# Two queues and some row operations rearranged in a graph-attention and top-p diffusion kernel

## The chip, the cores and the metric

The kernel runs on one core of a Trainium2 chip. A core has a matrix engine (PE, with its weight loads shown apart as PEld), a vector engine (DVE), an activation engine (ACT), a general-purpose engine (POOL, also called GpSimd) and SP, which here only issues transfers. Each engine takes its instructions from its own queue in order, and a wait of one instruction holds what stands behind it. The metric is device time in microseconds (us) of one execution; the median of several runs is compared.

## The reference

There are N = 4096 nodes with 256 features and a dense 0/1 matrix `adj`. Layer 0 is a graph attention layer of four heads; layer 1 is a diffusion with two operators, a fixed graph walk R and an attention that keeps the largest probabilities of each row until they sum to 0.9. Both are applied to the normalised input and added to it:

```python
R = S + jnp.eye(N)
R = R / R.sum(-1, keepdims=True)
Z = jnp.zeros_like(X); Xf = X; Xa = X
for n in range(2):
    A = _top_p_attention(Xa, W1, W2, W3)
    Xf = R @ Xf
    Xa = A @ Xa
    Z = Z + Xf @ U1[n].T + Xa @ U2[n].T
h = X + Z
...
return (h - mu) / jnp.sqrt(var + LN_EPS) * ln_g + ln_b

# around it
h = jnp.maximum(_layernorm(x), 0.0)
x = x + _L0_gnn_ref(h, adj, W, a, gamma, beta)
h = jnp.maximum(_layernorm(x), 0.0)
x = x + _L1_gnn_ref(h, adj, W1, W2, W3, U1, U2, ln_g, ln_b)
```

The final result is the layer-0 output x (called x1 in the kernel) plus the normalised h times `ln_g` plus `ln_b`.

## The kernel before

The nodes form NB = 32 row blocks of 128. The program's order is written out by hand: in each `manual_schedule` every engine's instructions stand in the order of the source, so what precedes what on a queue can be read off the code.

**Layer 0** (to about 780 us) makes the projections of all blocks and then 16 passes, one for each group of G0 = 8 blocks and each head. After the last head of a group comes `closing` (L495): statistics, then `close(i)` once per block, then `relu`, one piece at a time between the pair products of later passes (and, for the last group, between the first products of hop 1). `close` normalises the attention output into a tile `ob`, adds it to the block of `X` on DVE (L512) and stores `X` to `x1_d` from POOL's queue (L513). `ob` shares two buffers with `hb` of the prologue. POOL also adds `beta_r` to each block once (L627).

**Hop 1 and hop 2** are the products R @ Xf with the graph matrix, 128 products each (four passes of 32). `order[n]` names the n-th. For each one the kernel needs a row block, split into a high and a low part by ACT and DVE (`split`, L467 and L468, five buffers `hl`), and the matching edges (`edge`, L482, 512 KB from `adj_d`, issued by SP, five buffers). `graph_products` (L646) then issues eight matmuls of 512 columns. In hop 1 the rows are in `X`; in hop 2 `source` (L454) loads them from `xf_d`, 128 KB each, from POOL's queue (L461), into three buffers `x1` and two `xa`. `hops` (L687) lays this out: at its n-th turn it calls `source(n + 2)`, `edge(n)`, `split`, `own` and the products n - 5. `begin` does the first five of hop 2 while step 1's last block is still attended.

Hop n+1 is interleaved with two generators: `fills` makes the projections of step n (`projections`, L777), the first three blocks' exponentials (L947) and their probes (L954, then `first_step`, L968, some 20 one-column operations on POOL ending in `c3`, L997 or L1000), and `picks` does these blocks' searches on DVE (L1009, L1033 to L1052).

In the second step `projections` also calls `carried` for every block (L791): four matmuls (L797) make the products of the states with both U2 matrices; ACT copies the first half to a tile `part` (L799) and stores it in `v_d` from its own queue (L800), and DVE copies the second half into `X` (L801). `z_d` holds what step 1 left of Z plus X (stored by `finish`, L1311).

**Each step's loop** attends the blocks in turn. For block b, `chosen_kept(b)` (L1408) issues, engine by engine, the search for the threshold (DVE), `polished(b - 3)` (L1332, L1333 on POOL, store by SP), the third probe of b + 1 (L1015 on DVE, which needs `c3`), `finish(b - 2)` and `finish_scale(b - 2)` (L1313 and the statistics on DVE, L1320 to L1324 on POOL), `first_step(b + 2)`, `gathered(b - 1)` (three row operations on POOL, L1150 to L1152), `masked(b)` (L1058 on DVE), and `normal(b - 2)` on ACT. Then `began` loads a swapped copy of the queries by SP, `loads(b)` (L1109) loads xf, v, z and x1 of the block by SP, and `attend` (L1154) issues PE's work: the logits of block b + 3 (L763), 32 transposes (L1124, copied by ACT in L1126), 32 accumulations (L1132), and the product with U1 (L1142). The last three blocks have no logits to make. In step 1 the same loop runs with fewer row operations: `gathered`, `polished` and `normal` act in step 2 alone.

Of the kernel before, what the change touches and what calls it, by code (L numbers as in the profile page):

```python
# [11 lines left out]
F32 = mybir.dt.float32  # L12
# [10 lines left out]
ALU = mybir.AluOpType  # L23
# [3 lines left out]
P = 128  # L27
# [13 lines left out]
G0 = 8  # L41
# [15 lines left out]
def gat_then_top_p_diffusion(  # L57
# [18 lines left out]
    nc = tc.nc  # L76
    N, D = x.shape
    HD = a.shape[0] // 2
    H = D // HD
    DA = w2_t.shape[0]  # L80
    NB = N // P
    KC = D // P
# [32 lines left out]
    z_d = dram.tile([NB, P, D], F32, name="z_d")  # L115
    v_d = dram.tile([NB, P, D], F32, name="v_d")
# [45 lines left out]
    with tc.tile_pool(name="l0", bufs=1) as l0, tc.tile_pool(name="l0s", bufs=2) as l0s, tc.tile_pool(name="l0o", bufs=1) as l0o:  # L162
# [26 lines left out]
        with tc.manual_schedule(engines=every | {ET.SP}):  # L189
# [5 lines left out]
                nc.sync.dma_start(X[:, ts(g, 4), :], x[ts(g, 4 * P), :].rearrange("(b p) d -> p b d", p=P))  # L195

            nc.sync.dma_start(X[:, 0, :], x[:P, :])
            spots = l0.tile([P, KC, 2, H], F32, name="spots")
            nc.vector.memset(spots, 0.0)
            twice = l0.tile([2, 2, HD], F32, name="twice")  # L200
            nc.scalar.dma_start(twice, bass.AP(tensor=a.tensor, offset=a.offset, ap=[[HD, 2], [0, 2], [1, HD]]))
            nc.sync.dma_start(wx[:, :, :D], w.rearrange("(k p) d -> p k d", p=P))
            nc.sync.dma_start(X[:, 1:4, :], x[P:4 * P, :].rearrange("(b p) d -> p b d", p=P))
# [11 lines left out]
            slots = [t[:, i, :].bitcast(BF16).rearrange("p (h t w) -> p h t w", h=H, t=2) for t in slots for i in range(t.shape[1])]  # L215
            for t in slots:
                nc.gpsimd.memset(t[:, :, :, W3:], 1.0)
            roomy = l0o.tile([P, G0, D], F32, name="o").rearrange("p a b -> p (a b)")
            sr0 = l0s.tile([P, G0 * P], F32, name="sr")
            UV = 2 * H * W1  # L220
            uvs = [roomy[:, ts(i, UV)] for i in range(3)] + [l0s.tile([P, G0 * P], F32, name="sr")[:, :UV],
# [17 lines left out]
            def opened(b):  # L239
                if b < NB:  # L240
                    rs, nmr = pro.scales[b // 4] if b > 3 else pro.first
                    hb = pro.hb[b] = l0s.tile([P, D], F32, name="hb", tag="ob")
                    nc.scalar.activation(hb, X[:, b, :], AF.Relu, scale=rs[:, b % 4:b % 4 + 1], bias=nmr[:, b % 4:b % 4 + 1])

            def turned_rows(b):
# [208 lines left out]
        def source(A, n):  # L454
            if n in A.src or n >= len(order):
                return
            if A.hop == 0:
                A.src[n] = X[:, order[n][1], :]
            else:
                A.src[n] = S.rows.tile([P, D], F32, name="x1", bufs=3) if n % 5 < 3 else S.rows.tile([P, D], F32, name="xa")  # L460
                nc.gpsimd.dma_start(A.src[n], xf_d[order[n][1]])  # L461

        def split(A, n):
            while A.parted < min(n, len(order)):
# [30 lines left out]
        def closing(ig):  # L495
            o = out_rows[ig]
            mv = l0s.tile([P, G0, nc.vector.BN_AGGR_DIM], F32, name="mv8")
            scales = []

            def stats(i0):  # L500
                for i in range(i0, i0 + 2):
                    moments_of(mv[:, i, :], o[:, i, :])
                if i0 == G0 - 2:
                    scales.extend(steps(mv, G0, l0s))

            def close(i):
                b = ig * G0 + i
                xb = X[:, b, :]
                ob = l0s.tile([P, D], F32, name="ob")
                nc.scalar.activation(ob, o[:, i, :], AF.Identity, scale=scales[0][:, i:i + 1], bias=scales[1][:, i:i + 1])  # L510
                nc.vector.tensor_mul(ob, ob, gamma_r)
                nc.vector.tensor_add(xb, xb, ob)  # L512
                nc.gpsimd.dma_start(x1_d[b], xb)  # L513
                moments_of(mv[:, i, :], xb)
                if i == G0 - 1:
                    steps(mv, G0, l0s, x_rs[:, ts(ig, G0)], x_nmr[:, ts(ig, G0)])

            def relu(i0):
                for b in range(ig * G0 + i0, ig * G0 + i0 + 2):
                    nc.scalar.activation(X[:, b, :], X[:, b, :], AF.Relu, scale=x_rs[:, b:b + 1], bias=x_nmr[:, b:b + 1])  # L520
            return [lambda i=i: stats(i) for i in range(0, G0, 2)] + [lambda i=i: close(i) for i in range(G0)] \
                + [lambda i=i: relu(i) for i in range(0, G0, 2)]
# [254 lines left out]
    def projections(cur, n, G):  # L777
# [10 lines left out]
        lengths = small.tile([P, NB, 2], F32, name="lengths", bufs=1)  # L788
        u2 = S.u2.pop() if n > 0 else None

        def carried(xs, g, i):  # L791
            if n == 0:
                return
            b = 4 * g + i
            pt = ps3.tile([P, 4, P], F32, name="tp").rearrange("p a b -> p (a b)")
            for k in range(KC):
                nc.tensor.matmul(pt, xs[:, k, i, :], u2[:, k].rearrange("p n m -> p (n m)"), start=(k == 0), stop=(k == KC - 1))  # L797
            v = rows.tile([P, D], F32, name="part", bufs=3)
            nc.scalar.copy(v, pt[:, :D])  # L799
            nc.scalar.dma_start(block(v_d, b), v)  # L800
            nc.vector.tensor_copy(cur[:, b, :], pt[:, D:])  # L801

        for g in range(NB // 4):
            xs = l1e.tile([P, 3, 4, P], F32, name="xs", tag="e1")
# [301 lines left out]
    def block(t, b):  # L1106
        return t[ds(b, 1)].rearrange("o p d -> (o p) d")

    def loads(r):  # L1109
        r.xf, r.part = rows.tile([P, KC, P], F32, name="xf"), rows.tile([P, D], F32, name="part", bufs=3)  # L1110
        nc.sync.dma_start(r.xf, xft_d[r.n][ds(r.b, 1)].rearrange("o p s i -> (o p) s i"))
        if r.n > 0:
            r.v = rows.tile([P, D], F32, name="xa")
            nc.sync.dma_start(r.v, block(v_d, r.b))
            nc.sync.dma_start(r.part, block(z_d, r.b))
            r.x1 = rows.tile([P, D], F32, name="x1", bufs=3)
            nc.sync.dma_start(r.x1, block(x1_d, r.b))
        r.acc = ps1.tile([P, 2, D], F32, name="acc")
        r.far = r.acc[:, 1, :]
# [27 lines left out]

    def gathered(r):
        if r.n + 1 == STEPS:
            nc.gpsimd.tensor_tensor(r.part, r.part, r.v, ALU.add)  # L1150
            nc.gpsimd.tensor_tensor(r.x1, r.x1, ln_b_r, ALU.add)
            nc.gpsimd.tensor_tensor(r.part, r.part, r.xf.rearrange("p k i -> p (k i)"), ALU.add)  # L1152

    def attend(r, cur, ahead, between={}, eT=()):  # L1154
# [175 lines left out]
    def polished(r):  # L1330
        if r.n + 1 == STEPS:
            nc.gpsimd.tensor_tensor(r.part, r.part, ln_g_r, ALU.mult)  # L1332
            nc.gpsimd.tensor_tensor(r.part, r.part, r.x1, ALU.add)  # L1333
            nc.sync.dma_start(block(out.rearrange("(b p) d -> b p d", p=P), r.b), r.part)
# [48 lines left out]
    for n in range(STEPS):  # L1383
        cur = X
# [3 lines left out]
        with tc.manual_schedule(engines=every):  # L1388
# [19 lines left out]
            def chosen_kept(b):  # L1408

                r = blocks[b]  # L1410
                if not hasattr(r, "kept"):
                    candidates(r, found)
                if b > 2:
                    polished(blocks.pop(b - 3))
                if b + 1 < NB and not hasattr(blocks[b + 1], "thirded"):
                    third_probe(blocks[b + 1])
                if b > 1:
                    finish(blocks[b - 2])
                    finish_scale(blocks[b - 2])
                if b + 2 < NB and not hasattr(blocks[b + 2], "stepped"):  # L1420
                    first_step(blocks[b + 2])
                if 0 < b < NB - 1:
                    gathered(blocks[b - 1])
                if not hasattr(r, "kept"):
                    masked(r)
                if 1 < b < NB - 1:
                    normal(blocks[b - 2])
# [77 lines left out]
```

## Time and profile before

| | |
|---|---|
| median of 3 runs | 2851.52 us (2849.42 to 2852.96) |
| the profiled execution | 2851.36 us, its span 2849.5 us |
| mean granted PE clock | 0.994 |
| busy: DVE, ACT, POOL, share of the span | 76%, 67%, 34% |
| transfers | 376.43 MB, mean 132 GB/s |

```profile
PE   6999999999999999999999999999899999999998
DVE  9867878878554485888888887343565999999997
ACT  8867977879533727777887773233427778887782
POOL 7311121111010321333223331111524766666664
DMA  9969596786376881000000002767891111111110
```

Each digit is the busy share, in tenths, of one of 40 equal slices of 71 us. Layer 0 fills about the first eleven, hop 1 the next four and a half, step 1's loop runs to the 25th, hop 2 takes the next five, and step 2's loop the rest. The transfers tell the stages apart: the loops move little, the hops much.

```profile
ar<-adj_d SPq DMA_DIRECT2D x212, 512.0 KB, 4.5
x<-xf_d POOLq DMA_DIRECT2D x78, 128.0 KB, 4.6
xa<-xf_d POOLq DMA_DIRECT2D x50, 128.0 KB, 4.6
v_d<-part ACTq DMA_DIRECT2D x32, 128.0 KB, 2.3
```

These are issues by line: destination and source, the queue, the count, the size of one and the median time from issue to landing in us.

### The profile page before, as it was taken

Reading aid. Unit: us, or ns where it says so; the run is one execution under the profiler, and the core shown is the slowest. Engines: PE = TensorE matmul, PEld = TensorE weight load, DVE = VectorE, ACT = ScalarE, POOL = GpSimd, SP = SyncE. Lnnn points to the kernel's source line nnn. Section 1 sums busy time; section 2 is a strip of 40 time slices with the busy share of each in tenths; the row PEclk is TensorE's granted clock in tenths of the full one; section 3 lists DMA queues with packets and bytes.
Section 4 is the critical chain, followed back from the end, with each engine's and each line's share of the span. In section 5 each row is a group of like instructions: output and inputs, shape, how many; then the busy total and the mean of one; then the engine's idle time right before and its main releaser. Section 6 shows DMA issues by size and latency. Waiting matters only on the chain. (4 is left out here: it accounts for less than half of the span.)

```text
span 2849.5 us, 51595 instructions
## 1 busy us (share of the span) xinstructions
PE 2794.6 (98%) x18791; PEld 2439.9 (86%) x18791; DVE 2174.8 (76%) x5067; ACT 1917.7 (67%) x3066; POOL 980.9 (34%) x2023
## 2 busy tenths in 40 slices
PE   6999999999999999999999999999899999999998
PEld 5899999999988888888888888667678888888887
DVE  9867878878554485888888887343565999999997
ACT  8867977879533727777887773233427778887782
POOL 7311121111010321333223331111524766666664
PEclk9999999999999999999999999999999999999999
DMA  9969596786376881000000002767891111111110
GB/s 208 261 234 203 215 239 183 226 187 237 116 259 200 261 303 48 25 23 20 20 20 24 23 19 82 240 194 256 272 341 47 31 36 37 31 31 31 36 35 26
DMA packets 161825, 376.43 MB, mean 132 GB/s; under 512 B 18198, under 2 KB 107158, under 8 KB 157462
## 3 DMA queue, kind: packets, MB, share of 16 engines
q1 hardware_dynamic: 124064, 254.33, 27.0%
q0 software_dynamic: 32256, 114.31, 15.5%
q10 hardware_dynamic: 5238, 4.35, 0.5%
q8 instruction: 153, 2.51, 0.4%
q14 instruction: 114, 0.93, 0.1%
HBM read 305.48 MB, written 113.57 MB: 147 GB/s over the span
## 5 line engine op out<-in xcount | busy, mean ns | idle before, releaser
L1132 PE MATMUL acc<-X,eT 128*128 128x256 f32 x4096 | 971.7, 382 | 3.6 <-ACT eT L1126 3.1
L1132 PEld LDWEIGHTS acc<-X,eT 128*128 128x128 f32 x4096 | 738.2, 190 | 111.4 <-ACT eT L1126 31.9
L400 PE MATMUL acc<-ut,m 128*128 128x195 bf16 (+1 forms) x8192 | 698.1, 246 | 1.2 <-DVE m L379 0.9
L400 PEld LDWEIGHTS <-m 128*128 128x128 fp8e4 x8192 | 696.8, 97 | 2.4 <-DVE m L379 1.4
L372 ACT ACTIVATE g<-sr,d_big 128x1024 uint8<-128x1024 f32 x448 | 473.1, 1135 | 10.0 <-DVE m L378 10.0
L947 ACT ACTIVATE e<-mm,nm 128x1024 f32<-128x1024 f32 x256 | 286.3, 1119 | 195.8 <-PE mm L763 195.4
L1126 ACT COPY eT<-tp 128x512 f32<-128x512 f32 x512 | 297.1, 581 | 90.2 <-PE tp L1124 89.8
L1033 DVE MAX8 cand<-big 128x8 f32<-128x228 f32 (+1 forms) x1152 | 348.3, 380 | 0.0
L646 PE MATMUL mm<-ar,hl 128*128 128x512 f32 x848 | 337.7, 409 | 9.7 <-ACT hl L467 3.9
L1015 DVE SCALAR_TENSOR_TENSOR big<-e,c 128x4096 f32<-128x4096 f32 x58 | 261.9, 4515 | 97.6 <-POOL c L1000 58.6
L646 PE MATMUL acc<-ar,hl 128*128 128x512 f32 x848 | 325.3, 394 | 0.0
L1124 PE MATMUL tp<-ident,e 128*128 128x128 f32 x2048 | 306.1, 272 | 1.9 <-DVE ns_i_u L920 1.0
L1124 PEld LDWEIGHTS tp<-ident,e 128*128 128x128 f32 x2048 | 254.8, 140 | 61.2 <-DVE ns_i_u L920 1.3
L378 DVE TENSOR_TENSOR m<-g,ax 128x512 uint32<-128x512 uint32 x256 | 188.8, 737 | 97.3 <-PE acc L400 76.8
L1058 DVE SCALAR_TENSOR_TENSOR e<-e,found 128x4096 f32<-128x4096 f32 x58 | 259.1, 4468 | 0.0
L954 ACT ACTIVATE void<-e,c 128x2048 int8<-128x2048 f32 x128 | 257.5, 2012 | 0.0
L954 ACT ACTIVATE void<-e,c1x 128x2048 int8<-128x2048 f32 x128 | 257.4, 2011 | 0.0
L646 PEld LDWEIGHTS mm<-ar,hl 128*128 128x128 f32 x848 | 160.3, 189 | 50.3 <-issue 10.9
L379 DVE TENSOR_TENSOR m<-m,ax 128x512 uint32<-128x512 uint32 x256 | 183.2, 716 | 25.7 <-PE acc L400 0.5
L763 PE MATMUL mm<-kT,qT 128*128 128x512 f32 x512 | 197.9, 467 | 2.2 <-ACT e L947 2.2
L646 PEld LDWEIGHTS acc<-ar,hl 128*128 128x128 f32 x848 | 160.0, 189 | 36.7 <-issue 4.1
L971 POOL TENSOR_TENSOR sums<-sums 128x2 f32<-128x2 f32 x64 | 12.8, 200 | 511.1 <-ACT void L954 511.1
(313 smaller groups left out, 3610.9 us busy)
## 6 DMA issues: line engine op xcount, KB each, us to landing
ar<-adj_d SPq DMA_DIRECT2D x212, 512.0 KB, 4.5
adj_d<-ax POOLq DMA_DIRECT2D x32, 2048.0 KB, 7.7
ut<-uv_d SPq DMA_DIRECT2D x60, 784.0 KB, 6.1
aru<-adj_d SPq DMA_DIRECT2D x44, 512.0 KB, 4.5
ax<-in_adj_t_dram POOLq DMA_DIRECT2D x32, 512.0 KB, 18.3
x<-xf_d POOLq DMA_DIRECT2D x78, 128.0 KB, 4.6
xf<-xft_d SPq DMA_DIRECT2D x64, 128.0 KB, 2.2
sr<-s_d SPq DMA_DIRECT2D x15, 512.0 KB, 4.8
```

The costliest lines, as they stand in the source:

```text
L372: nc.scalar.activation(g[:, c, :], shared[k].sr, AF.Relu, scale=BIG, bias=d_big[:, h, j:j + 1])
L400: nc.tensor.matmul(shared[k].acc[i][:, t, :cols], m[t][:, c, ts(i, P)], shared[k].ut[j // QUARTER][:, j % QUARTER, t, :cols], start=(j == ...
L646: nc.tensor.matmul(A.acc[c][s], A.hl[m][:, t, ts(s, P)], A.ar[m][:, ts(c, 512)], start=(j == 0 and t == 0), stop=(j == NB - 1 and t == 1))
L763: nc.tensor.matmul(pm[:, h, :], q[t], kT[:, ds(h * (N // 2) + c * 512, 512)], start=(t == 0), stop=(t == 1))
L947: nc.scalar.activation(ev[:, :, c, :], r.pm[c], AF.Exp, bias=r.nm, accum_out=r.sums[:, c // 2, c % 2:c % 2 + 1])
L954: nc.scalar.activation(void, r.e[:, ts(h, N // 2)], (AF.Relu, AF.Sign)[i], bias=r.c1, scale=-1.0, accum_out=r.sums[:, h, 2 + i:3 + i])
L1015: nc.vector.scalar_tensor_tensor(big, r.e, r.c3, r.e, ALU.is_le, ALU.mult, accum_out=r.low3)
L1033: nc.vector.max(cand[:, s, :], big[:, edges[s]:edges[s + 1]])
L1058: nc.vector.scalar_tensor_tensor(r.e, r.e, r.t, r.e, ALU.is_ge, ALU.mult, accum_out=kept)
L1124: nc.tensor.transpose(pt[:, i, :], r.e[:, ts(4 * g + i, P)], ident)
L1126: nc.scalar.copy(eT, pt)
L1132: nc.tensor.matmul(r.acc[:, 0, :], eT[:, i, :], cur[:, j, :], start=(j == 0), stop=(j == NB - 1))
```

## The change

The rows of hop 2 are loaded from SP's queue instead of POOL's. `carried` loads the block's z ahead (two blocks early, from POOL's queue) and adds it on DVE to the first half, so that `v_d` holds v + z; its store moves from ACT's queue to POOL's, and the copy of the second half from DVE to ACT. `loads` then fetches one tile less. `close` adds `ln_b_r` on POOL, into `ob`, and stores that, so `gathered` keeps one of its three operations. `ob` and `hb` get four buffers; `spots` and `twice` move into tiles that are there anyway. In `chosen_kept`, `polished(b - 3)` moves behind `finish_scale(b - 2)`.

```diff
-            spots = l0.tile([P, KC, 2, H], F32, name="spots")
+            roomy = l0o.tile([P, G0, D], F32, name="o").rearrange("p a b -> p (a b)")
+            spots = roomy[:, G0 * D - 2 * KC * H:].rearrange("p (c t h) -> p c t h", c=KC, t=2)
...
-            twice = l0.tile([2, 2, HD], F32, name="twice")
+            twice = sT[:2].rearrange("t (r d) -> t r d", r=2)
@@ opened
-                    hb = pro.hb[b] = l0s.tile([P, D], F32, name="hb", tag="ob")
+                    hb = pro.hb[b] = l0s.tile([P, D], F32, name="hb", tag="ob", bufs=4)
@@ source
-                nc.gpsimd.dma_start(A.src[n], xf_d[order[n][1]])
+                nc.sync.dma_start(A.src[n], xf_d[order[n][1]])
@@ close
-                ob = l0s.tile([P, D], F32, name="ob")
+                ob = l0s.tile([P, D], F32, name="ob", tag="ob", bufs=4)
...
-                nc.gpsimd.dma_start(x1_d[b], xb)
+                nc.gpsimd.tensor_tensor(ob, xb, ln_b_r, ALU.add)
+                nc.gpsimd.dma_start(x1_d[b], ob)
@@ projections
+        zs = {}
+
+        def fetched(b):
+            if n > 0 and b < NB:
+                zs[b] = rows.tile([P, D], F32, name="z", tag="xf")
+                nc.gpsimd.dma_start(zs[b], block(z_d, b))
+
+        for b in range(2):
+            fetched(b)
@@ carried
-            nc.scalar.copy(v, pt[:, :D])
-            nc.scalar.dma_start(block(v_d, b), v)
-            nc.vector.tensor_copy(cur[:, b, :], pt[:, D:])
+            nc.vector.tensor_tensor(v, pt[:, :D], zs.pop(b), ALU.add)
+            nc.gpsimd.dma_start(block(v_d, b), v)
+            fetched(b + 2)
+            nc.scalar.copy(cur[:, b, :], pt[:, D:])
@@ loads
-            r.v = rows.tile([P, D], F32, name="xa")
-            nc.sync.dma_start(r.v, block(v_d, r.b))
-            nc.sync.dma_start(r.part, block(z_d, r.b))
+            nc.sync.dma_start(r.part, block(v_d, r.b))
@@ gathered
-            nc.gpsimd.tensor_tensor(r.part, r.part, r.v, ALU.add)
-            nc.gpsimd.tensor_tensor(r.x1, r.x1, ln_b_r, ALU.add)
             nc.gpsimd.tensor_tensor(r.part, r.part, r.xf.rearrange("p k i -> p (k i)"), ALU.add)
@@ chosen_kept
-                if b > 2:
-                    polished(blocks.pop(b - 3))
...
                     finish(blocks[b - 2])
                     finish_scale(blocks[b - 2])
+                if b > 2:
+                    polished(blocks.pop(b - 3))
```

More of the change, by code (lines that the diff above doesn't have):

```diff
@@ L217, in gat_then_top_p_diffusion @@
                 nc.gpsimd.memset(t[:, :, :, W3:], 1.0)
-            roomy = l0o.tile([P, G0, D], F32, name="o").rearrange("p a b -> p (a b)")
             sr0 = l0s.tile([P, G0 * P], F32, name="sr")
```

## The prediction

> **What bounds the kernel now.** I read the page's busy table and its 40 slices first, then the windows of the slices where PE is not full, then the timelines of PE, ACT and POOL inside them, and last the groups by shape in the two long loops. PE carries the span: 98% busy, and nearly full in all but a few places.
>
> ```profile
> PE 2794.6 (98%) x18791; PEld 2439.9 (86%) x18791; DVE 2174.8 (76%) x5067; ACT 1917.7 (67%) x3066; POOL 980.9 (34%) x2023
> ```
>
> The largest hole lies in hop 2 (about 1778 to 2138 us). The windows view gives busy time and, in brackets, instructions started per stretch; then PEclk, DMA share and GB/s:
>
> ```profile
> 2020.00:2030.00 10.00, 10.00 (x45) 8.24 (x44) 8.22 (x25) 6.21 (x9) 8.76 (x20) 1.00 0.93 341
> 2030.00:2040.00 10.00, 5.17 (x19) 3.41 (x19) 5.09 (x22) 4.12 (x8) 3.89 (x11) 0.78 0.83 288
> 2040.00:2050.00 10.00, 6.64 (x24) 4.97 (x23) 2.73 (x15) 0.40 (x1) 6.69 (x15) 0.84 0.53 163
> 2050.00:2060.00 10.00, 9.44 (x30) 7.62 (x31) 9.35 (x17) 2.00 (x5) 2.73 (x5) 0.70 0.62 214
> 2060.00:2070.00 10.00, 10.00 (x45) 8.20 (x45) 9.50 (x27) 2.19 (x6) 3.28 (x6) 1.00 0.94 315
> ```
>
> A full stretch starts 45 matmuls; the three in the middle start 19, 24 and 30, and the granted clock falls with them. The timelines say who is late:
>
> ```profile
> 2028.02 0.63 POOL L461 DMA_DIRECT2D xa<-xf_d  x1
> 2033.59 0.40 ACT L467 CAST hl<-xa 128x256 fp32r<-128x256 f32 x1 [6.56 <-DMA xa<-xf_d]
> 2034.05 0.50 PE L646 MATMUL mm<-aru,hl 128*128 128x512 f32 x1 [1.80 <-ACT hl L467]
> ...
> 2036.91 0.20 POOL L971 TENSOR_TENSOR sums<-sums 128x2 f32<-128x2 f32 x1 [1.62 <-ACT void L954]
> 2044.66 1.72 POOL L461 DMA_DIRECT2D x<-xf_d  x3
> 2049.39 0.40 ACT L467 CAST hl<-x 128x256 fp32r<-128x256 f32 x1 [9.73 <-DMA x<-xf_d]
> 2050.56 0.77 PE L646 MATMUL mm<-ar,hl 128*128 128x512 f32 x1 [3.92 <-ACT hl L467]
> ```
>
> POOL runs the small operations of `first_step` (L971 to L997) from 2018.95 to 2027.9 and again from 2036.91 to 2044.6; the row loads L461 stand behind them in POOL's queue, ACT then waits 6.56 and 9.73 us for rows, and PE for ACT.
>
> The two loops over 32 row blocks are another matter. Their L1142, once per block, comes every 22.30 us in step 1 and every 22.26 us in step 2, although DVE has 47.2 us of waits for POOL over 25 blocks of step 1 (1.9 us each) and none in step 2. So PE sets both. In step 2 DVE only looks like the bound (the chain of waits follows it there): L1058 ends 2.96 us before PE takes its result, block after block. What fills it shows in the groups of step 1 (1150 to 1700 us), then of step 2 (2200 to 2750 us):
>
> ```profile
> L1045 DVE TENSOR_TENSOR_SCAN cum<-best,cum,zero 128x48 f32<-128x48 f32 x24 | 7.7, 321 | 0.9
> L1050 DVE CUSTOM_DVE_ANT_0 work<-drop,best 128x48 f32<-128x48 f32 x24 | 6.4, 268 | 0.8
> L1049 DVE TENSOR_SCALAR drop<-cum 128x48 f32<-128x48 f32 x24 | 4.6, 194 | 0.8
> ...
> L1050 DVE CUSTOM_DVE_ANT_0 work<-drop,best 128x48 f32<-128x48 f32 x25 | 19.2, 768 | 0.9
> L1045 DVE TENSOR_TENSOR_SCAN cum<-best,cum,zero 128x48 f32<-128x48 f32 x25 | 16.5, 659 | 0.9
> L1049 DVE TENSOR_SCALAR drop<-cum 128x48 f32<-128x48 f32 x25 | 14.2, 570 | 0.9
> ```
>
> The same three operations cost 0.78 us in step 1 and 2.00 in step 2, where POOL's five row operations (0.73 us each) run beside them.
>
> **What the Trainium skill says.** SBUF — State Buffer, "SBUF: two separate sides": VectorE and GpSimd share a port pair under an exclusive lock, and the loser blocks for the whole instruction. The trace agrees both ways: the groups above, and POOL's one-column L1320, which takes 4.36 us while L1058 (4.45 us) runs. DMA: Bandwidth & Descriptors, "Issuing engines are not separate DMA queues": moving a DMA to another issuer saves only the issuer's time, as all run on the same 16 engines. So I count nothing for bandwidth, only for the place in the queue. The same page, "Latency and other measured facts", puts the first byte of a DMA issued by SP or ACT near 0.6 us and of GpSimd's near 1 us; here SP's 128 KB loads land in 2.2 us in step 2 and POOL's in 3.4 (median, 1780 to 1925 us) to 5.2 (2000 to 2125 us), but under different load.
>
> **The change part by part.** *Row loads of hop 2 on SP.* 128 of L461 leave POOL. From 2031.5 to 2062 PE starts 73 matmuls; at its steady 0.2275 us (2062 to 2086: 105 in 24 us) these take 16.6 us, so 13.9 us were lost. On SP row n+2 stands ahead of the edges of n and behind those of n-1, which wait for product n-6. It is used at product n+2, so it has 7 products, 12.7 us at 8 x 0.2275 each, for landing, ACT (0.41) and DVE (0.42). POOL gave it some 15 us less whatever `first_step` took. I take the 13.9 us as won. The new wait ahead of an edge load is split n-3 on DVE (L468), 4.5 us earlier than the edge's own wait for product n-5; DVE's pieces there are at most 2.35 us (L1009), so it mostly hides. What is late next is the DMA: a product needs 640 KB, 360 GB/s at full rate, where 341 to 400 GB/s is what such stretches move; from 2086 to 2098, 43 matmuls took 12 us instead of 9.8, on edges. I keep that 2.2 us, and charge 1.0 for its spreading (0 to 4; if the whole stretch to 2098 ran at that 0.279 us, 178 x 0.0515 = 9.2).
>
> At the start of hop 2 the move costs. Before, POOL sent rows 5 to 7 at 1773.6 to 1776.3; now they follow edge 5 (1784.49), with the X load and row 8, before edge 6. Four issues at 0.43 put edge 6 1.7 us later, and PE uses it at about 1792, where its landing was the last wait. Charge 2.0 (0.5 to 3.5).
>
> *z joined to the states' products.* 32 copies on ACT (L799, 0.37) become 32 additions on DVE, nearest row L1313, 0.48; DVE's copy (L801, 0.43) goes to ACT. The store moves from ACT (L800, 0.34 of issue) to POOL, with 32 new z loads; the z loads of step 2 and 32 v loads vanish. PE is full from 1800 to 1925 with DVE at about 40% and ACT at 30%: nothing on the path. A new wait: the addition needs z, and behind it on DVE stand the hop's L468. z of b+2 is issued after addition b: 0.48 + 2 x 0.54 + 3.4 = 5.0 us, where two blocks of PE take 8.2 (four take 16.45) and the tightest pair 6.65. Cost 0 (0 to 3 for single late landings).
>
> *ln_b in layer 0.* 32 additions on POOL, 0.74 each (L627 is the same shape), and the store reads `ob`, of which there are now four. POOL is busy 5 to 25% there, its closings have 1.24 us of idle time per block even in the last eight (799 to 812 us), and DVE, which they can block for 0.74 us, is under 60% busy in that stretch while PE is 49.3 to 50 of 50 us busy. Cost 0 (-0.5 to +1). `spots` and `twice` only change places: 0.
>
> *Step 2's loop.* POOL loses two row operations a block (L1150, L1151: 1.46 us), and L1332 and L1333 move ahead of `first_step`, beside L1033. There DVE should not be blocked: L1040, the same operation, kept 0.31 us beside L1150. DVE gains up to 1.2 us a block, but PE paces, so 28 blocks give 0. `first_step` starts about 1 us later, with 4.3 us to spare before L1015. The out store and the next q and block loads behind it on SP come some 12 us later; q is used a block later and xf at the block's end (20 us on), so 0. At the end, where blocks 29 to 31 have no logits and PE needs 18.7 us, DVE is late today: PE waits 0.84 us for L1058, and 1.04 and 0.65 for eT where step 1 shows 0.29. With DVE ahead that is 0.84 + 0.75 + 0.36 = 1.95 us. Take 2.0 (0.8 to 2.2).
>
> **Sum.** 13.9 - 1.0 - 2.0 + 2.0 = 12.9 us off. The profiled execution took 2851.4 us (span 2849.5); the median of the runs is 2851.5, so both say **2838.5 us**. With all bounds good (13.9 + 2.2 - 0.5 + 2.2 + 0.5) it is 2833; with all bad (13.9 - 4 - 3.5 + 0.8 - 4) 2848.
>
> **Rivals.**
> *The transfers take over.* Rows and edges in one queue, at 360 GB/s wanted, run at the rate of 2086 to 2098: the 9.2 us above instead of 1.0, so 2846.7. For it: DMA share 0.93 to 1.03 from 2060 to 2120. Against: PE started 45 or 46 in most of these stretches all the same.
> *Nothing is won in hop 2*, as SP's in-order queue waits on DVE's splits and edges come late as rows did: only the tail's 2.0 less the start's 2.0, so 2851.5. Against: 4.5 us of slack.
> *Slower: the z loop.* If a z load lands in L, two blocks take 1.56 + L; from L = 6.7 it is slower than PE's 8.2, and at about 7.5 it eats all the gain. At L = 8.5 it costs 0.92 x 32 = 29 us, so 2868. For it: one row load of POOL landed in 6.6 there, and under 2000 to 2125's load up to 8.5. Against: the median of 3.4.
> *The DVE slack counts in the loop:* if PE did follow DVE in step 2, 28 x 1.2 = 34 us would go (2805). Step 1, where DVE waits and PE's period is the same, speaks against it.
>
> **How the numbers follow.** Forecast 0.76; transfers 0.10; nothing won 0.03; z loop 0.08; loop follows DVE 0.03. The range 2831 to 2847 holds most of the forecast with its bounds, and the transfers' case. A change under 0.2% (5.7 us, so from 2845.8 up) can't be told from none. Faster is 0.75 of the forecast (0.01 lies in its bad end), 0.06 of the transfers' case and the loop's 0.03: 0.84. Same: 0.01, 0.04 and 0.02 of nothing won, 0.07. Slower: the z loop and 0.01 of nothing won, 0.09.
>
> **What would show it.** Right: no ACT wait for a row over 2 us in hop 2, PEclk 1.00 in its slices, 45 matmuls per 10 us, L1142 still every 22.26 to 22.30 us, L1049 near 0.2 us, DVE waiting for L997. Wrong: PE idle for edges, L468 waiting behind a z, a loop period under 22.2.

## The result, and the profile after

| | before | after |
|---|---|---|
| median (lowest to highest) | 2851.5 us (2849.4 to 2855.6), 6 runs | 2840.0 us (2838.8 to 2842.5), 6 runs |
| ratio, 95% interval | | 0.996 (0.9947 to 0.9972) |
| span of the profiled execution | 2849.5 us | 2837.2 us |
| mean granted PE clock | 0.994 | 0.996 |

The change takes off 11.5 us, where 12.9 were forecast. To find where, I compare positions in the two traces. They are start times of single matmuls, in us from the start of the span; the last column is what the stretch since the row above gained (+) or lost (-).

| matmul | before | after | stretch |
|---|---|---|---|
| first product of layer 0 (L400) | 79.64 | 80.08 | -0.44 |
| last product of hop 1 | 1072.91 | 1075.09 | -1.74 |
| first product of hop 2 | 1778.03 | 1779.92 | +0.29 |
| last product of hop 2 | 2137.84 | 2126.89 | +12.84 |
| U1 product of block 28 in step 2's loop (the fourth last) | 2782.03 | 2770.87 | +0.21 |
| U1 product of block 31 | 2835.32 | 2822.74 | +1.42 |
| end of the span | 2849.50 | 2837.18 | -0.26 |

Hop 2 gained 12.84 us and the tail 1.42; layer 0 with hop 1 lost 1.74. The 0.44 at the very start is not from the change: the kernel with the row loads alone, whose layer 0 is that of before, has its first product at 80.12.

The busy table of the page after:

```profile
PE 2790.7 (98%) x18791; PEld 2438.5 (86%) x18791; DVE 2155.8 (76%) x5067; ACT 1915.4 (68%) x3066; POOL 915.8 (32%) x1927
```

POOL has 96 instructions fewer: 128 row loads and 64 row operations are gone, 64 z loads and v stores and 32 row operations came. PE is still the bound, and the hole in hop 2 is filled. These are the windows of after (columns as in the prediction: stretch, PE, PEld, DVE, ACT, POOL, PEclk, DMA share, GB/s):

```profile
2030.00:2040.00 10.00, 10.00 (x46) 8.21 (x45) 8.05 (x33) 3.92 (x7) 6.81 (x20) 1.00 0.95 336
2040.00:2050.00 10.00, 10.00 (x45) 8.23 (x44) 9.66 (x25) 2.44 (x6) 0.19 (x1) 1.00 1.01 375
2050.00:2060.00 10.00, 10.00 (x45) 8.23 (x44) 10.00 (x26) 2.04 (x5) 0.00 (x0) 1.00 1.02 353
```

Where before started 19, 24 and 30 matmuls, after starts 46, 45 and 45, at full clock. The waits view of ACT in after from 2000 to 2070 us (engine, line, releaser: total, times, longest):

```profile
ACT hl L467 <- DMA x<-xf_d: 13.0, 10, 2.3
...
ACT hl L467 <- DMA xa<-xf_d: 6.3, 5, 1.7
```

The longest wait for a row in this stretch is 2.3 us, where it was 9.7. ACT still waits 15 times for rows, but PE is busy all through 2020 to 2060 us, so each row arrives before PE asks for it. `first_step` still keeps POOL busy (6.8 us of 10 in 2030 to 2040), and no row load stands behind it. The transfers themselves did not get faster: the page after has a median of 5.1 us from issue to landing, where POOL's loads took 4.6.

In step 2's loop the groups of after (2200 to 2750 us; POOL's L1009 makes `c3`) show DVE's three small operations back at step 1's price, 2.00 us down to 0.80, and the third probe L1027 now waiting for POOL and lasting longer:

```profile
L1027 DVE SCALAR_TENSOR_TENSOR big<-e,c 128x4096 f32<-128x4096 f32 x25 | 122.9, 4914 | 17.7 <-POOL c L1009 17.7
L1057 DVE TENSOR_TENSOR_SCAN cum<-best,cum,zero 128x48 f32<-128x48 f32 x24 | 7.9, 330 | 0.9
L1062 DVE CUSTOM_DVE_ANT_0 work<-drop,best 128x48 f32<-128x48 f32 x24 | 6.4, 268 | 0.8
L1061 DVE TENSOR_SCALAR drop<-cum 128x48 f32<-128x48 f32 x24 | 4.7, 197 | 0.8
```

The period of the loop, from U1 product to U1 product, is 22.26 us before and 22.25 after.

### The profile page after: what moved, and what is told of

Same layout as the page of the kernel before. It is cut to its first block, busy times and chain, and to the rows that moved or that the text cites. A ratio compares the mean times of both kernels' runs of the same rounds, so it can differ in the third digit from the quotient of the medians.

```text
span 2837.2 us, 51681 instructions
## 1 busy us (share of the span) xinstructions
PE 2790.7 (98%) x18791; PEld 2438.5 (86%) x18791; DVE 2155.8 (76%) x5067; ACT 1915.4 (68%) x3066; POOL 915.8 (32%) x1927
## 5 line engine op out<-in xcount | busy, mean ns | idle before, releaser
L400 PE MATMUL acc<-ut,m 128*128 128x195 bf16 (+1 forms) x8192 | 698.1, 246 | 1.2 <-DVE m L379 0.9
L400 PEld LDWEIGHTS <-m 128*128 128x128 fp8e4 x8192 | 696.8, 97 | 2.4 <-DVE m L379 1.5
L1027 DVE SCALAR_TENSOR_TENSOR big<-e,c 128x4096 f32<-128x4096 f32 x58 | 272.6, 4701 | 118.0 <-POOL c L1012 58.5
```

The lines of the kernel that those rows point to most:

```text
L400: nc.tensor.matmul(shared[k].acc[i][:, t, :cols], m[t][:, c, ts(i, P)], shared[k].ut[j // QUARTER][:, j % QUARTER, t, :cols], start=(j == ...
L1027: nc.vector.scalar_tensor_tensor(big, r.e, r.c3, r.e, ALU.is_le, ALU.mult, accum_out=r.low3)
```

## The experiments

My theory after the result: (a) the whole gain of hop 2 comes from taking the row loads out of POOL's queue, where they stood behind `first_step`; (b) hop 1's loss comes from the ln_b edit, against the prediction's zero; (c) the start of hop 2 loses because rows stand behind an edge load; (d) the loop's period belongs to PE; (e) the tail's gain comes from row operations taken off POOL. The rivals stand in each expectation. All twelve runs stand in one table beside before and after: "to hop 1's end" is from the first product of layer 0 to the last of hop 1, "hop 2" from its first to its last product, "tail" from the U1 product of block 28 to that of block 31.

| kernel | median us (lowest to highest) | ratio to before, 95% | to hop 1's end | hop 2 | tail |
|---|---|---|---|---|---|
| before | 2851.5 (2849.4 to 2855.6) | | 993.27 | 359.81 | 53.29 |
| after | 2840.0 (2838.8 to 2842.5) | 0.9947 to 0.9972 | 995.01 | 346.97 | 51.87 |
| rows_alone | 2839.8 (2839.3 to 2842.6) | 0.9949 to 0.9975 | 992.55 | 346.74 | 54.94 |
| rows_back | 2852.3 (2849.5 to 2857.7) | 1.0001 to 1.0013 | 994.95 | 359.39 | 51.87 |
| close_back | 2838.2 (2836.5 to 2839.4) | 0.9942 to 0.9967 | 993.46 | 347.64 | 51.87 |
| step_on_dve | 2844.6 (2842.0 to 2846.4) | 0.9968 to 0.9985 | 992.75 | 351.79 | 53.27 |
| store_from_x | 2839.2 (2838.4 to 2839.4) | 0.9945 to 0.9972 | 993.96 | 347.26 | 51.87 |
| polished_back | 2839.8 (2838.7 to 2842.0) | 0.9950 to 0.9977 | 994.73 | 347.63 | 51.88 |
| rows_first | 2837.7 (2837.0 to 2840.4) | 0.9941 to 0.9969 | 995.72 | 347.43 | 51.87 |
| z_one_ahead | 2874.9 (2874.2 to 2878.2) | 1.0073 to 1.0104 | 995.49 | 382.23 | 51.87 |
| after_again | 2840.5 (2839.4 to 2841.5) | 0.9949 to 0.9976 | 994.84 | 347.88 | 51.88 |
| best_sp | 2836.4 (2835.7 to 2837.2) | 0.9935 to 0.9962 | 992.79 | 345.26 | 51.87 |
| best_pool | 2836.1 (2835.2 to 2839.0) | 0.9936 to 0.9963 | 992.86 | 345.64 | 51.88 |
| z_back | 2839.8 (2838.7 to 2841.2) | 0.9945 to 0.9973 | 995.46 | 348.26 | 51.88 |

The intervals of most versions overlap; the columns by stage, one profile each, are what separates them. In these columns the two profiles of the same changed kernel, after and after_again, differ by 0.2, 0.9 and 0.0 us.

### One part alone, and one part undone: the rows' queue

```diff
 rows_alone (on the kernel before)
-                nc.gpsimd.dma_start(A.src[n], xf_d[order[n][1]])
+                nc.sync.dma_start(A.src[n], xf_d[order[n][1]])
```

> The kernel before with one line changed: the row loads of hop 2 go on SP's queue instead of POOL's. My theory (the rows stood behind first_step in POOL's queue): hop 2, from its first to its last matmul, falls from 359.8 us to about 347 as in the changed kernel, and nothing else moves, so 2851.5 - 12.8 = 2838.7 us (2837.5 to 2840.5), with 45 matmuls per 10 us from 2020 to 2060 us. Rival, the z join carries a part of it (ACT and its queue relieved of 32 copies and stores in hop 2): hop 2 stays 3 us or more above 347, time above 2841.5.

```diff
 rows_back (on the kernel after)
-                nc.sync.dma_start(A.src[n], xf_d[order[n][1]])
+                nc.gpsimd.dma_start(A.src[n], xf_d[order[n][1]])
```

> The changed kernel with the row loads of hop 2 back on POOL's queue, the rest as changed. My theory: hop 2 takes at least 359.8 us again and the time is 2840.0 + 12.8 = 2852.8 us or more, since z loads and v stores now share that queue with the rows; the tail's gain and the loss in hop 1 stay. Rival, the rows' queue was only one of several gains: time under 2848.

Measured: one line alone gives hop 2 in 346.74 us, the changed kernel's 346.97, and undoing that line gives 359.39. The z join carries nothing of it. Taken from these two kernels, the one line is worth 12 to 13 us of hop 2. The time of rows_alone is 1.1 us over the middle of the expectation and within its range; in its profiled execution the tail lost 1.65 us to the clock (the last section). rows_back comes 0.4 us short of the least that I had expected of hop 2, and 0.5 us short in time, less than its runs differ. In it the rows are late in the same way; the timelines of POOL and ACT, where the hop's cast waits 8.59 us for a row that POOL issues after `first_step`'s last operation:

```profile
2047.59 0.34 POOL L1009 TENSOR_SCALAR c<-fell,c,up 128x1 f32<-128x1 f32 x1
2048.03 1.72 POOL L461 DMA_DIRECT2D x<-xf_d  x3
...
2051.46 0.40 ACT L467 CAST hl<-x 128x256 fp32r<-128x256 f32 x1 [8.59 <-DMA x<-xf_d]
```

### The same queue, without what stood in front

This separates "behind `first_step`" from "POOL's way of sending DMAs is slow". The rows stay on POOL; `first_step` leaves it in hop 2 (`inverse` is DVE's reciprocal there, and the power of 1/e becomes an exponential on ACT).

```diff
 step_on_dve (on the kernel before)
-    def first_step(r):
+    def first_step(r, pool=nc.gpsimd):
...
-                first_step(blocks[b - 1])
+                first_step(blocks[b - 1], nc.vector if n > 0 else nc.gpsimd)
...
-        pool.tensor_tensor(d, d, mone, ALU.pow)
+        inverse(d)
...
+            nc.scalar.activation(t, y, AF.Exp, scale=-1.0)
```

> The kernel before with the rows still on POOL's queue, but first_step's small operations in hop 2 on DVE (one of them, an exponential, on ACT; powers of -1 become reciprocals). My theory (what hurt was standing behind first_step in the queue): the stalls of 6.6 and 9.7 us on rows go, hop 2 shrinks by 9 to 13.9 us, the rest being DVE's longer queue, so 2838 to 2843 us. Rival, POOL's own way of issuing DMAs or their landing is what is late: hop 2 stays at 358 us or more, time 2850 or more.

Measured: hop 2 took 351.79 us, 8.0 less than before, with the rows on POOL; the two long waits for rows are gone. So position in the queue is the cause, not POOL's transfers. The 5 us that hop 2 still takes longer than with the rows on SP come from one stall, which the experiment made itself, and from the clock after it. The timeline of DVE and PE (L977 to L1007 are `first_step`'s operations there):

```profile
2032.41 0.15 DVE L977 TENSOR_TENSOR sums<-sums 128x2 f32<-128x2 f32 x1
...
2035.43 0.27 DVE L1007 TENSOR_SCALAR c<-fell,c,den 128x1 f32<-128x1 f32 x1
...
2036.99 0.42 DVE L468 TENSOR_TENSOR hl<-x,hl 128x256 fp32r<-128x256 f32 x1
2037.71 0.77 PE L646 MATMUL mm<-ar,hl 128*128 128x512 f32 x1 [4.34 <-issue]
```

The hop's L468 stood behind 3.3 us of `first_step` and a piece of the search, and PE, which starts 0.3 us after L468 ends, waited 4.34 us: again work behind other work in a queue, now DVE's. The granted clock is 0.77 from 2030 to 2040 us and 0.89 in the next 10 us. The least of the expectation, 9 us off hop 2 and 2843 us, was missed by 1.0 and 1.6 us.

### Why hop 1 lost: the ln_b edit

```diff
 close_back (on the kernel after)
-                nc.gpsimd.tensor_tensor(ob, xb, ln_b_r, ALU.add)
-                nc.gpsimd.dma_start(x1_d[b], ob)
+                nc.gpsimd.dma_start(x1_d[b], xb)
...
         if r.n + 1 == STEPS:
+            nc.gpsimd.tensor_tensor(r.x1, r.x1, ln_b_r, ALU.add)
```

> The changed kernel without the ln_b edit of layer 0: the closed rows are stored from X again, and ln_b is added to x1 on POOL in step 2, as before; spots and twice stay where the change put them. My theory: the 1.7 us that hop 1 lost come back (its matmuls from the last closings on run as before), and the third row operation on POOL in step 2 costs nothing since PE paces the loop: 2840.0 - 1.7 = 2838.3 us. Rival, the loss comes from the moved buffers or the loads, not from the closings: 2840.0, with PE still idle 2.5 us between 810 and 820 us. A second rival, POOL's extra row operation beside the third probe matters after all: 28 x 0.7 = 20 us slower.

```diff
 store_from_x (on the kernel after)
-                nc.gpsimd.dma_start(x1_d[b], ob)
+                nc.gpsimd.dma_start(x1_d[b], xb)
```

> The changed kernel with one word changed: the store of the closed rows in layer 0 reads X and not ob, while POOL still makes the addition of ln_b into ob; so the stored rows lack ln_b, and the work is the same. In the changed kernel ACT waits 4.34, 1.32 and 1.40 us there for a store out of ob to land, with the hop's hl casts behind it, and DVE's L468 takes 0.52 us instead of 0.39 beside POOL. If the held buffer is what cost hop 1 its 1.7 us: ACT's waits for the store go, 2840.0 - 1.5 = 2838.5 us, as with close_back. If POOL's addition, slowing DVE, is the cost: 2840.0, PE's gaps of 1.0 and 1.4 us stay.

Measured: close_back ends hop 1 after 993.46 us, as before. Over all runs the seven kernels with the whole edit lie at 994.73 to 995.72 (mean 995.2), the six without it at 992.55 to 993.46 (mean 993.0): the edit costs 2.2 us. Both rivals of close_back fall. The loop of step 2 kept its 22.25 us with a second row operation in `gathered`, although POOL's L1160 takes 4.91 us there (0.91 in after) and DVE waits 14.7 us for it over 25 blocks.

The mechanism, first in lines of before that were not shown, then in after. These are the last closing's statistics on DVE and the scales that POOL works out from them, and in after the products' wait as well. In before no product waits for a cast there:

```profile
812.28 0.18 DVE L150 BATCH_NORM_AGGREGATE mv<-st 128x2 f32<-128x6 f32 x1
812.70 0.24 POOL L141 TENSOR_SCALAR x_rs<-mv 128x8 f32<-128x8 f32 x1
815.09 0.20 POOL L144 TENSOR_TENSOR x_nmr<-x_nmr,x_rs 128x8 f32<-128x8 f32 x1
```

```profile
803.77 0.74 POOL L513 TENSOR_TENSOR ob<-X,ln_b_r 128x256 f32<-128x256 f32 x1 [0.31 <-DVE X L512]
804.28 0.52 DVE L468 TENSOR_TENSOR hl<-X,hl 128x256 fp32r<-128x256 f32 x1
...
813.83 0.18 DVE L150 BATCH_NORM_AGGREGATE mv<-st 128x2 f32<-128x6 f32 x1
814.45 0.56 POOL L514 DMA_DIRECT2D x_d<-ob  x1 [0.30 <-POOL ob L513]
815.09 0.23 POOL L141 TENSOR_SCALAR x_rs<-mv 128x8 f32<-128x8 f32 x1
817.48 0.21 POOL L144 TENSOR_TENSOR x_nmr<-x_nmr,x_rs 128x8 f32<-128x8 f32 x1
817.72 1.09 ACT L521 ACTIVATE X<-X,x_nmr,x_rs 128x256 f32<-128x256 f32 x2 [5.00 <-POOL x_nmr L144]
819.16 0.50 PE L647 MATMUL mm<-ar,hl 128*128 128x512 f32 x1 [1.44 <-ACT hl L467]
```

The closings are one serial chain: in these two profiles DVE has no gap over 0.11 us in them, and after the eighth POOL's scales release the ReLU on ACT, its casts, and PE. From 780 to 900 us PE is idle for 1.27 us in before and 3.00 in after, at a clock of 1.00, which accounts for the loss of 1.74 us of this pair. A wait for an edge ahead of it varies by run and shortens the wait for the cast: they are 1.04 and 1.44 us in after, 0.22 and 2.03 in after_again. Beside POOL's addition DVE's L468 takes 0.52 us instead of 0.39, so a block takes 1.91 us instead of 1.78; and the last addition with its store stands on POOL ahead of L141, which starts 1.08 us after L150 ends, where it was 0.24. The Trainium skill (SBUF — State Buffer, "Who interferes with whom") says just this of a VectorE instruction with two SBUF inputs beside a GpSimd instruction that reads SBUF; L468 and L513 are such a pair, and the trace agrees with 0.13 us.

store_from_x tells the addition from the buffer that the store holds. ACT's waits for the store went, as the first theory said, but L468 kept 0.52 to 0.59 us, and hop 1 ended after 993.96 us: 1.2 of 2.2 us came back, and PE still waited 1.01 us for a cast. I read the part from the chain itself. The eight closings take from the first L150 to the last 12.48 us without the edit, 13.48 in store_from_x and 13.30 to 14.74 with the whole edit (mean 13.95); from the last L150 to L144 it is 2.81, 3.38 and 3.65. So the addition alone costs the chain 1.0 + 0.6 us, where the whole edit costs 1.5 + 0.8 on the mean.

The other 0.7 us belong to the store, which there waits for the addition and holds the buffer, and they vary from run to run. In after and after_again DVE has no gap in the closings, and they take no longer than in store_from_x. In the other five profiles with the whole edit DVE has gaps of 0.23 to 1.38 us before L511, which needs the `ob` that ACT's L510 writes; L510 has to wait for a free one. In rows_first:

```profile
808.79 0.60 ACT L510 ACTIVATE ob<-o,nmr,rs 128x256 f32<-128x256 f32 x1 [2.87 <-DMA x_d<-ob]
809.43 0.42 DVE L511 TENSOR_TENSOR ob<-ob,gamma_r 128x256 f32<-128x256 f32 x1 [1.38 <-ACT ob L510]
```

Neither theory holds alone.

### Reordering and row operations: loop and tail

```diff
 polished_back (on the kernel after)
                     candidates(r, found)
+                if b > 2:
+                    polished(blocks.pop(b - 3))
                 if b + 1 < NB and not hasattr(blocks[b + 1], "thirded"):
...
-                if b > 2:
-                    polished(blocks.pop(b - 3))
                 if b + 2 < NB and not hasattr(blocks[b + 2], "stepped"):
```

> The changed kernel with polished issued again before the third probe, as in the kernel before; its two row operations on POOL then stand ahead of finish_scale. My theory: the loop of step 2 keeps its 22.25 us (PE paces), and in the tail DVE is kept ahead mostly by the two row operations that gathered lost, so the time stays within 0.7 us of 2840.0. Rival, the reordering carries the tail's gain: PE waits 0.8 us for the masked row at the second last block again, and 2840.0 + 1.4 = 2841.4 us. Second rival, POOL's place in the order decides the loop: over 2845.

Measured: the tail is 51.88 us, with the changed kernel's own waits, and the loop 22.26. So the tail's gain does not need the reordering; in the old order the row operations that left `gathered` are enough. In the new order one of the two is enough: close_back and z_back each put one back, so that `gathered` has two, and keep 51.87 and 51.88. Only the kernels with all three, before, step_on_dve and rows_alone, take 53.3 us or more, with DVE's masked row 0.8 us late. These three also have the old order; no run has all three operations in the new order, so what the order would do for the tail by itself is not shown.

### The z join

```diff
 z_back (on the kernel after)
-            nc.vector.tensor_tensor(v, pt[:, :D], zs.pop(b), ALU.add)
-            nc.gpsimd.dma_start(block(v_d, b), v)
-            fetched(b + 2)
-            nc.scalar.copy(cur[:, b, :], pt[:, D:])
+            nc.scalar.copy(v, pt[:, :D])
+            nc.scalar.dma_start(block(v_d, b), v)
+            nc.vector.tensor_copy(cur[:, b, :], pt[:, D:])
```

(and the loads of v and z and their addition in step 2 as before)

> The changed kernel without the z join: ACT copies v out and stores it, DVE copies the other half, and v and z are loaded apart and added on POOL in step 2. My theory: hop 2 stays within 0.7 us of 347 (the join costs and gains nothing there), the loop keeps 22.25 us, and with two row operations in gathered the tail still has DVE ahead, as it had without the ln_b edit: 2840.0 us within 0.8. Rival, the join carries the tail's gain: 2841.4. Second rival, the additions on DVE cost hop 2 time: under 2838.5.

```diff
 z_one_ahead (on the kernel after)
-        for b in range(2):
-            fetched(b)
+        fetched(0)
...
-            fetched(b + 2)
+            fetched(b + 1)
```

> The changed kernel with z loaded one block ahead instead of two in the z join. This tests the mechanism of the slower rival: after the addition of block b, the store's issue and the load's issue (2 x 0.54), a landing of 3.4 us and the next addition (0.42 and the semaphores) make about 5.0 us a block, where PE gives a block 4.1 us in hop 2. If that chain paces: 32 x 0.9 = 29 us slower than the changed kernel, 2869 us, with DVE's L468 and so the products late. If other slack hides it: 2840 to 2845.

Measured: without the join hop 2 takes 348.26 us, 0.6 over the bound that I had set, with it 346.97 and 347.88, and the time is the same. So the join costs or gains nothing that these runs can tell from their spread. But it depends on its look-ahead of two. With one, hop 2 takes 35 us more. Windows of 1800 to 1925 us, z_one_ahead, then after:

```profile
1800.00:1925.00 125.00, 105.44 (x415) 71.45 (x413) 38.27 (x73) 27.29 (x65) 24.91 (x46) 0.89 0.60 187
```

```profile
1800.00:1925.00 125.00, 124.95 (x549) 85.88 (x548) 49.60 (x96) 37.56 (x89) 31.89 (x59) 1.00 0.75 238
```

And one turn of its timeline, from addition to addition 5.76 us:

```profile
1854.84 0.42 DVE L809 TENSOR_TENSOR part<-tp,z 128x256 f32<-128x256 f32 x1
...
1856.09 0.55 POOL L797 DMA_DIRECT2D z<-z_d  x1
1860.60 0.42 DVE L809 TENSOR_TENSOR part<-tp,z 128x256 f32<-128x256 f32 x1 [5.34 <-issue]
1861.48 1.11 PE L819 MATMUL tp<-ident,X 128*128 128x128 f32 x4 [4.48 <-ACT X L812]
```

The z load goes out after the addition of the block before, the next addition comes when it has landed, and PE waits for what ACT copies after that. The slower rival's mechanism is real. The estimate of 29 us was 6 short: it took 5.0 us for a turn where the additions come every 5.56 us on the mean (4.16 in after), and it counted no lower clock (0.89 here). In part of the turns the addition waits for PE's own product and not for z; what each of these adds is not separated.

### The start of hop 2, and versions that beat both

In the changed kernel rows 5 to 7 are sent at 1786.75, behind the load of edge 5, which waits for PE:

```profile
1786.37 0.33 SPq L482 DMA_DIRECT2D ar<-adj_d  x1
1786.75 1.37 SPq L461 DMA_DIRECT2D x<-xf_d  x3
1790.94 1.13 ACT L467 CAST hl<-x 128x256 fp32r<-128x256 f32 x3 [10.16 <-DMA x<-xf_d]
1791.39 0.51 PE L647 MATMUL mm<-ar,hl 128*128 128x512 f32 x1 [1.40 <-ACT hl L467]
```

The rows in turn stand ahead of edge 6, as the prediction said. Edge 6 is issued at 1785.42 in before and at 1789.25 in after. DVE's L490 on it waits for its landing, first in before, then in after:

```profile
1791.94 0.29 DVE L490 TENSOR_TENSOR ar<-ar,ident 128x128 fp32r<-128x128 f32 x1 [3.20 <-DMA ar<-adj_d]
```

```profile
1795.80 0.29 DVE L490 TENSOR_TENSOR ar<-ar,ident 128x128 fp32r<-128x128 f32 x1 [0.51 <-DMA ar<-adj_d]
```

Counted from the first product of hop 2 in each, edge 6 goes out 1.9 us later than before and is there 2.0 us later, and PE starts its product 0.04 us after L490 starts (1791.98 before, 1795.84 after). So this edge alone would hold PE about as long as the late rows do.

```diff
 rows_first (on the kernel after)
-                if n == A.begun:
-                    edge(A, n)
                 for i in range(3 if n == A.begun else 1):
```

> The changed kernel without the call that issues the fifth edge load ahead of rows 5 to 7 at the start of hop 2: SP sends these three rows first, and then the edge, which waits for the product of edge 0. My theory (the rows stood behind that edge's wait): SP was idle there, so rows land some 2 us earlier, PE's gaps of 1.4 and 0.9 us at 1791 to 1793 us go to about 0.3, and hop 2 is 2 us shorter: 2838.0 us (2837.3 to 2838.8). Rival, the transfers are what is late at that point: the rows gain, the edges lose as much, 2840.0.

Measured: from its first product on, the first 520 matmuls of hop 2 (65 products) take 224.69 us in before, 227.28 in after and 225.60 in rows_first. The start's cost is 2.6 us, and the order gives 1.7 of it back. It brings both the rows and edge 6 forward, so it does not say which of them held PE. One profile each leaves these numbers loose: the seven kernels with the changed start (z_one_ahead aside) take 226.16 to 227.52 us for these matmuls, which makes the cost 1.5 to 2.8, and the three with another order of rows 5 to 7 take 225.60 to 225.64. The rest of the hop took 2.1 us longer in that one profile, so that hop 2 as a whole stayed at 347.43; the median, 2.3 us under after's, lies within the spread of both. On its own this run is inconclusive. So the order was tried again in kernels whose layer 0 is that of before, with ln_b added in `gathered`. best_sp sends rows 5 to 7 first on SP, best_pool sends these three alone on POOL; after_again is the changed kernel itself.

```diff
 best_sp (on the kernel after)
-                if n == A.begun:
-                    edge(A, n)
 best_pool (on the kernel after)
-                nc.sync.dma_start(A.src[n], xf_d[order[n][1]])
+                (nc.gpsimd if 5 <= n < 8 else nc.sync).dma_start(A.src[n], xf_d[order[n][1]])
```

> The changed kernel once more, so that the next ones stand beside it on the same chip: 2840.0 us (2838.8 to 2841.2). By position in the trace, hop 1 should end 995 us after the first product of layer 0, give or take 0.6, and hop 2 last 346.7 to 347.7 us.

> The changed kernel with all its edits in layer 0 undone (the closed rows are stored from X, ln_b is added to x1 in step 2) and, at the start of hop 2, rows 5 to 7 sent on SP ahead of the fifth edge. My theory: the two costs of the change add up, about 2.0 us in hop 1 (995.1 against 993.1 us in the runs with and without the edit) and up to 1.7 us at the start of hop 2: 2840.0 - 3.7 = 2836.3 us. Rival, what the start gains is given back in the stretch of 2075 to 2090 us, where PE waits for edges: 2838.0, no better than without the ln_b edit.

> The changed kernel with all its edits in layer 0 undone and only the rows 5 to 7 of hop 2 back on POOL, which is free then and not behind SP's edge; all other rows stay on SP. My theory: the start of hop 2 runs as in the kernel before (2.6 us shorter than in the changed one), hop 1 is 2.0 us shorter: 2840.0 - 4.6 = 2835.4 us. Rival as with the SP order: the edges' transfers at 2075 to 2090 us take the start's gain back, 2838.0.

Measured on the same chip: 2840.5, 2836.4 and 2836.1 us. The runs of best_sp, 2835.7 to 2837.2, all lie under those of the changed kernel, 2839.4 to 2841.5. Both best versions end hop 1 after 992.8 us and take 225.6 us for the first 520 matmuls, and this time hop 2 as a whole kept the gain (345.3 and 345.6). In best_sp the casts of rows 5 to 7 no longer wait for the rows, and what PE waits for is the landing of edges:

```profile
1784.41 0.41 ACT L467 CAST hl<-x 128x256 fp32r<-128x256 f32 x1 [5.60 <-PE acc L646]
1792.28 0.47 PE L646 MATMUL mm<-ar,hl 128*128 128x512 f32 x1 [0.89 <-DMA ar<-adj_d]
```

POOL's queue for these rows is no better than SP's: from here the edges set the pace, and 1 us of the start's cost stays in both.

## Why the prediction was right, and where it was off

The forecast was 2838.5 us, 12.9 off; the runs give 2840.0, 11.5 off. The case was the likeliest one. The terms were off by more than the sum shows, in part against one another, so that the sum came this near is in part luck.

- **Rows on SP, 13.9 won less 1.0 for spreading.** Right in mechanism (rows_alone, rows_back, step_on_dve), too small in size: after its first 520 matmuls, hop 2 fell from 135.12 to 119.69 us, 15.4 won; over the eleven kernels with the rows on SP, one profile each, it is 13.3 to 15.5. The charge for the transfers' rate was not due. From 2020 to 2060 us PE starts 45 or 46 matmuls per 10 us at a DMA share of 0.95 to 1.02, and in place of the waits for edges that had cost 2.2 us from 2086 on there is one, of 1.17 us, at 2077. The rival that the transfers take over falls with it.
- **The start of hop 2, 2.0 lost.** Measured 2.6, within its bounds, and the reason I gave is there: edge 6 goes out 1.9 us later (I had 1.7) and PE takes it up as it lands. What I left out is the rows themselves, which stand behind edge 5's wait for PE: PE waits 1.40 us for them first. The two waits overlap, so the sum hardly changed; that was luck.
- **z join, 0.** Right as far as the spread of the runs tells, and with less margin than I had worked out: a turn of z_one_ahead takes 5.56 us on the mean where I had 5.0, against 8.2 us for two blocks of PE.
- **ln_b in layer 0, 0 (-0.5 to +1).** This step failed: 2.2 us, outside its bounds. I took POOL's idle 1.24 us per block and DVE's share of under 60% in 50 us as cover. Inside the eight closings of before DVE has no gap over 0.11 us, and POOL's last addition and store stand ahead of the scales that PE is waiting for through ACT. The share averaged the chain with the quiet stretch beside it.
- **The loop of step 2, 0.** Right in all twelve runs: 22.25 to 22.26 us, whether DVE's three small operations took 2.00 us or 0.80. In after DVE's gain turns into a wait for `c3` (17.7 us over 25 blocks, 0.7 each) and a longer third probe (4.91 us beside a POOL row operation, 4.52 before).
- **The tail, 2.0 (0.8 to 2.2).** Measured 1.42. The 0.84 us for the masked row went; of the eT waits 1.04 and 0.65, I had expected 0.29 each, and both are 0.65. Of the reason, that DVE gets ahead, the gone row operations are shown; the new order is not needed.

The sum with the measured terms, 15.4 - 2.6 - 2.2 + 1.4, is 12.0 us, and the medians differ by 11.5. Of the signs that I had named, one did not come: ACT still waits over 2 us for rows in hop 2, 10.16 us at its start and up to 2.9 later.

## What to carry to other kernels

A DMA that an engine issues waits for everything in front of it in that engine's queue, small operations and their waits included; here ACT waited 6.56 to 9.73 us for such loads. The Trainium skill (DMA: Bandwidth & Descriptors, "Issuing engines are not separate DMA queues") says that another issuer saves only the time to initiate, "usually small". For the transfers the trace agrees, as a row took 5.1 us to land from SP and 4.6 from POOL; but one line moved was worth 12 to 13 us, because of what stood before the loads. When loads change queue, check the new queue's waits in the same way. For an operation added beside a chain, look for gaps inside that chain, not at the busy share of the stretch around it; and before you count a faster engine's time as gained, find out which engine sets the period.

## What the runs showed of the hardware

I had not expected how much of a stall's price is the clock that follows it. In hop 2 of before, in windows of 5 us (the kernel before, three of seven between 2030 and 2065 us):

```profile
2035.00:2040.00 5.00, 1.97 (x7) 1.14 (x6) 4.53 (x21) 3.14 (x6) 2.82 (x9) 0.56 0.80 295
2040.00:2045.00 5.00, 5.00 (x18) 3.94 (x18) 2.56 (x14) 0.00 (x0) 4.23 (x11) 0.76 0.20 51
...
2050.00:2055.00 5.00, 4.44 (x11) 3.50 (x12) 5.00 (x9) 1.19 (x3) 1.64 (x3) 0.50 0.46 166
```

PE was idle 8.75 of these 35 us. The granted clock, taken over its busy time window by window, is another 5.0 us: 13.7 in all, near the 13.9 of the prediction. In z_one_ahead the clock's 0.89 over 105 busy us makes 11.6 us on top of 19.6 idle, most of the 35 that it lost.

Short stalls can do it too. In the tail of rows_alone PE waited 0.81 and 1.04 us within 2.1 us, and the next 3.4 us ran at half the clock (windows of rows_alone):

```profile
2788.50:2791.90 3.40, 1.57 (x10) 1.34 (x11) 3.37 (x12) 2.03 (x4) 3.21 (x6) 1.00 0.00 0
2791.90:2795.30 3.40, 3.40 (x11) 2.73 (x11) 3.37 (x15) 0.00 (x0) 1.80 (x3) 0.51 0.12 39
```

In before the same two waits, 0.84 and 1.04 us, were followed by a clock of 1.00, and its tail is 1.65 us shorter (windows of before; from 2800.20 to 2803.60 PE is busy for 2.56 us):

```profile
2803.60:2807.00 3.40, 2.35 (x14) 1.86 (x12) 3.40 (x13) 1.56 (x3) 3.24 (x6) 1.00 0.00 0
2807.00:2810.40 3.40, 3.40 (x21) 3.05 (x20) 3.23 (x15) 1.17 (x2) 0.50 (x1) 1.00 0.38 118
```

The Trainium skill (TensorE: Matmul & The Clock Gate, "Part 1: The HAM clock gate") has a free-running window of recent activity behind this, and the clock's records in the fourteen traces agree: in every record the clock is 1.0 or 0.5, and within a trace all its changes lie whole multiples of 3.41 us apart. On this grid, from 80 us on, a stretch at full clock was followed by one at half clock in 21 of the 22 cases in which PE was busy for less than half of it, and in none of the others. The windows above lie on this grid: in rows_alone both waits fall into one stretch, which leaves PE 46% busy (1.57 of 3.40 us), while in before the boundary at 2803.6 us parts them. So the price of equal stalls differs with where they fall on the grid.
